# Side products of a two-layer attention kernel in four column groups, with a new schedule for them

## The chip, the cores and the metric

The kernel runs on one core of a Trainium2 chip. The metric is the device time of one execution in microseconds (us). The core has a matrix engine (TensorE, PE in the profile, with its weight loads as PEld), a vector engine (VectorE, DVE), a scalar engine (ScalarE, ACT), a general engine (GpSimd, POOL), a queue engine that issues transfers (SyncE, SP), and 16 DMA engines. Matmul results go to PSUM, eight banks of 128 x 512 floats.

## The reference, cut to what matters

Two layers on x of shape (4, 256, 64, 64), all float32. Layer 0 ("A") is attention of every pixel to 1024 keys that come from 2x2 convolutions; layer 1 ("B") is attention within four areas of 1024 pixels each, plus a 7x7 depthwise convolution of the values, and a projection.

```python
# layer 0: x = x + L0(_gn(x));  8 heads of 32, scale 32**-0.5
q = einsum('oc,bchw->bohw', Wq, x)                  # 4096 queries an image
k, v = conv2x2_stride2(x, Wk), conv2x2_stride2(x, Wv)   # 1024 keys and values
attn = softmax((q.k + q.(rel_h + rel_w)) * scale);  out = attn @ v
# layer 1: x = x + L1(_gn(x))
q, k, v = conv1x1(x, w_qkv)                         # in 4 areas of 1024 pixels
out = softmax(q.k * scale) @ v                      # within an area
out = conv1x1(out + dwconv7(v, w_pe), w_proj)       # 49 taps
# _gn: normalization over 32 groups of channels, of the whole image
```

## The kernel before

The program is a list of 128 units in eight blocks of 16 (A of images 0, 1, 2, then B0, A3, B1, B2, B3). A unit is 512 queries of four heads. It has eight steps, one for each 128 keys. In each step TensorE makes the scores (`s`), ScalarE exponentiates them into two tiles `p`, and a step later TensorE adds up the weighted values in one bank (`av`). The four heads share the array: scores lie in four row groups (32 x 128), the sums of v and of the exponentials (`den`, the divisors) in four column groups (128 x 32).

```python
def weighted(unit, j, p, av):
    v = unit[3]()
    for h in range(4):
        T.matmul(
            av[HD * h : HD * h + HD, :], lhsT=v[:, j, unit[0] * P + HD * h : unit[0] * P + HD * h + HD],
            rhs=p[h // 2][:, h % 2, :], start=(j == 0), stop=(j == NKT - 1),
        )
```

All else TensorE does (keys, values and queries of both layers, the projection, the values for the convolution) is a side task. A task is a generator that yields after each piece of its matmuls; all of them use the full array (128 x 128). A piece is two matmuls of 512 columns or four of 256. Tasks take one of three pairs of banks (`s`) that the scores use too.

```python
def make_k(a, qd):                       # of layer 1; the others look alike
    ...
    k, ps = kvs["k"], ps_pair(f"k1ps_{b}_{a}_{qd}")
    for half in range(2):
        for t in range(CT):
            T.matmul(
                ps[:, half, :], lhsT=wqkv_sb[:, t, 1, qd * P : (qd + 1) * P],
                rhs=hs[a][:, t, half * CH : (half + 1) * CH], start=(t == 0), stop=(t == CT - 1),
            )
        if half == 0:
            yield
    S.activation(...)                    # PSUM to SBUF
```

The main loop. `advance()` runs one piece of the oldest task; `need()` runs pieces until a result that is wanted is there.

```python
while now[0] < last or plan or later or side:
    g, j = divmod(now[0], NKT)
    if now[0] < last:
        if j == 0:
            ps = {}
        ps[j] = scores(units[g], j)
    do(g, j)                             # what the plan has for this step; tasks go to side
    for _ in range(1 + (len(side) > 2)):
        if side:
            advance()
    if before is not None:
        weighted(*before)
        if j == 0:
            avs[g - 1] = pool.tile([P, CH], FP, tag="av", name="av_sb", bufs=2)
            S.copy(avs[g - 1], before[3])
    ...
```

The divisors: outside the time of the convolutions (`free`) VectorE adds all eight steps' exponentials and one divisor group follows in step 1 of the next unit. While VectorE works at the convolutions (units 22 to 123) it makes five adds a unit, GpSimd issues folding DMAs (`accum_op`), and three divisor groups follow in steps 1, 2 and 3.

```python
    free = g + 1 < begin or g > start
    if free:
        if j:
            add(0, 0, j)
            add(1, 0, j)
        groups = [(9, 0, 0)]
    else:
        if j % 2:
            fold(j - 1, j)
        if j == 3:
            soon(3, lambda: fold(0, 2))
        if j % 3:
            add(1, j - j % 3, j)
        groups = [(9, 0, 0), (10, 4, 3), (11, 6, 6)]
```

Dividing: the divisors are copied to `den_sb`, sent through memory into a narrow tile (`rows`, `few`), inverted there, sent back and spread (`recs`, `rb`), and multiplied over a unit later. The convolution is 49 multiply-adds on VectorE into one accumulator (`acc`, one buffer), for each of four images, two halves and two channel blocks, 6.3 units apart from unit 22.3 on. ScalarE normalizes in `normalize`, VectorE gathers statistics with bn_stats. x is read in chunks of 512 KB: once for the statistics (`xs`), again for keys and values (`xa`), for queries (`hq`) and for the residual (`xc`).

Of the kernel before, what the change touches and what calls it, by code (L numbers as in the profile page):

```python
# [15 lines left out]
P = 128  # L16
B, C, HH, WW = 4, 256, 64, 64
N = HH * WW
CT = C // P
# [31 lines left out]
def direct_path(  # L51
# [50 lines left out]
    S.dma_start(wv0_sb, wv0.rearrange("(t p) k o -> p t k o", p=P))  # L102
    S.dma_start(wq0_sb, wq0.rearrange("(t p) o -> p t o", p=P))
    relh_sb = const.tile([P, CT, 32], FP, name="relh_sb")
    relw_sb = const.tile([P, CT, 32], FP, name="relw_sb")
    S.dma_start(relh_sb, relh.rearrange("(t p) j -> p t j", p=P))
    S.dma_start(relw_sb, relw.rearrange("(t p) j -> p t j", p=P))
    G.dma_start(wqkv_sb, wqkv.rearrange("(t p) k o -> p t k o", p=P))
    G.dma_start(wp_sb, wproj.rearrange("(t p) o -> p t o", p=P))
    wpe_sb = const.tile([P, CT, NTAP], FP, name="wpe_sb")  # L110
    G.dma_start(wpe_sb, wpe.rearrange("(t p) k -> p t k", p=P))
    bqkv_sb = const.tile([P, 3, CT], FP, name="bqkv_sb")
    G.dma_start(bqkv_sb, bqkv.rearrange("k (t p) -> p k t", p=P))
    bpe_sb = const.tile([P, CT], FP, name="bpe_sb")
    G.dma_start(bpe_sb, bpe.rearrange("(t p) -> p t", p=P))
    bproj_sb = const.tile([P, CT], FP, name="bproj_sb")
    G.dma_start(bproj_sb, bproj.rearrange("(t p) -> p t", p=P))

    bpv_sb = const.tile([P, CT], FP, name="bpv_sb")
    V.tensor_add(bpv_sb, bpe_sb, bqkv_sb[:, 2, :])  # L120
# [169 lines left out]
    def plan_a(b, u, prep):  # L290
# [4 lines left out]
        seen = {}  # L295

        def look(c):
            seen[c] = first[c] if b == 0 and c < len(first) else load_chunk(b, c, "xs")

        def add_stats(c):  # L300
            for t in range(CT):
# [21 lines left out]
        def make_k(a):  # L323
            if a == 0:
                taps["k"] = k_tile(key)
            k, ps = taps["k"], ps_pair(f"k0ps_{b}_{a}")
            for qd in range(2):
                for n in range(8):
                    t, i, w = n // 4, n // 2 % 2, n % 2
                    T.matmul(  # L330
                        ps[:, qd, :256], lhsT=wk0_sb[:, t, 2 * i + w, qd * P : (qd + 1) * P],
                        rhs=taps[a][:, t, i, w], start=(n == 0), stop=(n == 7),
                    )
                    if n == 3 or n == 7 and qd == 0:
                        yield
            S.copy(k[:, :, a * 256 : (a + 1) * 256], ps[:, :, :256])  # L336
            if a == NAREA - 1:

                for qd in range(2):
                    rows = k[:, qd, :].rearrange("p (i j) -> p i j", j=32)  # L340
                    V.tensor_add(rows, rows, relh_sb[:, qd : qd + 1, :].to_broadcast([P, 32, 32]))
                    V.tensor_add(rows, rows, relw_sb[:, qd, :].unsqueeze(2).to_broadcast([P, 32, 32]))
                ks[key] = k

        def make_v(a):
            if a == 0:
                taps["v"] = v_tile(key)
            v, ps = taps["v"], ps_pair(f"v0ps_{b}_{a}")
            for m in range(2):
                for n in range(8):  # L350
                    t, i, w = n // 4, n // 2 % 2, n % 2
                    T.matmul(  # L352
                        ps[:, m, :C], lhsT=taps[a][:, t, i, w, m * P : (m + 1) * P],
                        rhs=wv0_sb[:, t, 2 * i + w, :], start=(n == 0), stop=(n == 7),
                    )
# [26 lines left out]
        def make_q(c):  # L382
            hq = hqs.pop(c)
            q = pool.tile([P, 2, CH], FP, tag="q", name=f"q0_{b}_{c}", bufs=2)
            ps = ps_pair(f"q0ps_{b}_{c}")
            for qd in range(2):
                for t in range(CT):
                    T.matmul(  # L388
                        ps[:, qd, :], lhsT=wq0_sb[:, t, qd * P : (qd + 1) * P], rhs=hq[:, t, :],
                        start=(t == 0), stop=(t == CT - 1),  # L390
                    )
                if qd == 0:
                    yield
            S.copy(q, ps)  # L394
            qs["A", b, c] = q
# [33 lines left out]
    def plan_b(b, u):  # L429
# [14 lines left out]
        def make_k(a, qd):  # L444
            if qd == 0:
                kvs["k"] = k_tile(("B", b, a))
            k, ps = kvs["k"], ps_pair(f"k1ps_{b}_{a}_{qd}")
            for half in range(2):
                for t in range(CT):
                    T.matmul(  # L450
                        ps[:, half, :], lhsT=wqkv_sb[:, t, 1, qd * P : (qd + 1) * P],
                        rhs=hs[a][:, t, half * CH : (half + 1) * CH], start=(t == 0), stop=(t == CT - 1),
                    )
                if half == 0:
                    yield
            S.activation(
                k[:, qd, :].rearrange("p (h n) -> p h n", h=2), ps, AF.Identity, bias=bqkv_sb[:, 1, qd : qd + 1]
            )
            if qd == 1:
                ks["B", b, a] = k  # L460

        def make_v(a, half):
# [4 lines left out]
            for m in range(4):  # L467
                kt = 4 * half + m
                for t in range(CT):
                    T.matmul(  # L470
                        ps[:, m, :], lhsT=hs[a][:, t, kt * P : (kt + 1) * P],
                        rhs=wqkv_sb[:, t, 2, :], start=(t == 0), stop=(t == CT - 1),
                    )
# [6 lines left out]
        def make_q(c):  # L480
            q = pool.tile([P, 2, CH], FP, tag="q", name=f"q1_{b}_{c}", bufs=2)
            ps = ps_pair(f"q1ps_{b}_{c}")
            for qd in range(2):
                for t in range(CT):
                    T.matmul(  # L485
                        ps[:, qd, :], lhsT=wqkv_sb[:, t, 0, qd * P : (qd + 1) * P],
                        rhs=hs[c // 2][:, t, (c % 2) * CH : (c % 2 + 1) * CH],
                        start=(t == 0), stop=(t == CT - 1),
# [30 lines left out]
        def project(c):  # L519
            cv, xm = rest[c]  # L520
            ps = ps_pair(f"ops_{b}_{c}")
            for to in range(CT):
                for t in range(CT):
                    T.matmul(  # L524
                        ps[:, to, :], lhsT=wp_sb[:, t, to * P : (to + 1) * P], rhs=cv[:, t, :],
                        start=(t == 0), stop=(t == CT - 1),
                    )
# [28 lines left out]
    def plan_values(b, c, start):  # L556
# [11 lines left out]
        def values():  # L568
            h = made.pop("h")
            ps = ps_pair(f"vals_ps_{b}_{c}")  # L570
            for t in range(CT):
                for tt in range(CT):
                    T.matmul(  # L573
                        ps[:, t, :], lhsT=wqkv_sb[:, tt, 2, t * P : (t + 1) * P], rhs=h[:, tt, :],
                        start=(tt == 0), stop=(tt == CT - 1),
                    )
# [11 lines left out]
    def plan_conv(b, half, t, start, pace):  # L588
# [58 lines left out]
    for b in range(B):  # L647
        assert start >= ends[b] + 6.0
        for c in range(NCH):
            plan_values(b, c, start - 3.7 + 0.4 * c if c < 5 else start + 3.0 * (c - 4))  # L650
        for half in range(2):
            for t in range(CT):
                plan_conv(b, half, t, start, pace)
# [19 lines left out]
        tc.manual_schedule(engines={engines.PE, engines.Activation, engines.DVE, engines.Pool, engines.SP})  # L673
    )

    def sum_up(g, j, ps):
# [3 lines left out]
        free = g + 1 < begin or g > start  # L680
        if free:

            if j:
                add(0, 0, j)
                add(1, 0, j)
# [18 lines left out]
    while now[0] < last or plan or later or side:  # L704
# [629 lines left out]
```

## Time and profile before

| | before |
|---|---|
| time, median of three runs | 3722.2 us (3713.27 to 3727.89) |
| span in the profile | 3716.5 us |
| instructions | 55404 |
| first scores of unit 0 start at | 94.4 us |
| last copy of a sum of v (av_sb) starts at | 3676.6 us |
| last copy of divisors (den_sb) starts at | 3680.9 us |

How to read it: the page gives each engine's busy time and its share of the span. A group is one line of the program with one pair of tiles; its mean is that of one instruction. A float32 matmul appears as two instructions (two passes), so eight `av` instructions are the four heads of one step. Matmuls overlap, so their durations don't add up: what a group costs is read from its start to the next group's start. The costliest groups, as line, engine, operation, tiles, count, busy us and mean ns, and the idle time before them:

```profile
L237 ACT ACTIVATE p<-s 128x1024 f32<-128x1024 f32 x2048 | 1991.2, 1026 | 968.5 <-PE s L232 794.9
L616 DVE SCALAR_TENSOR_TENSOR acc<-vin,wpe_sb,acc 128x1984 f32<-128x1984 f32 (+12 forms) x768 | 1714.0, 2232 | 6.3
L678 DVE TENSOR_TENSOR p<-p 128x1024 f32<-128x1024 f32 x874 | 1045.2, 1220 | 322.4 <-PE av L244 147.0
L679 POOL DMA_DIRECT2D p<-p x510 | 445.0, 930 | 2513.6 <-ACT p L237 778.2
L470 PE MATMUL v1ps<-wqkv_sb,h 128*128 128x256 f32 x512 | 128.3, 394 | 0.0
L573 PE MATMUL vals_ps<-hv,wqkv_sb 128*128 128x512 f32 x256 | 126.8, 618 | 1.2 <-ACT p L237 0.8
```

The first is ScalarE's exponentials, the second VectorE's taps, the third its adds, the fourth the folding DMAs. The last two are two of the eight kinds of side products.

### The profile page before, as it was taken

To read this page: it belongs to the slowest core of one execution; us is meant where nothing else is said; L and a number is where in the kernel's file an instruction comes from. 1 tells how busy PE (TensorE), PEld (TensorE's weight loads), DVE (VectorE), ACT (ScalarE), POOL (GpSimd) and SP (SyncE) were. 2 spreads that over 40 slices of the span, in tenths; PEclk is the share of its full clock that TensorE was granted. 3 is DMA by queue.
4 is the path that set the end of the run, shared out by engine and by line. 5 is a ranking of instruction groups with operands and counts; after the bars stand their busy time and mean duration, and the time that the engine had idled before them with its cause. 6 is when DMAs were issued, how large, how long until landed. Compare 5 with 4: busy or idle time off the path is not lost.

```text
span 3716.5 us, 55404 instructions
## 1 busy us (share of the span) xinstructions
PE 3536.4 (95%) x21890; PEld 1136.7 (31%) x21890; DVE 3030.7 (82%) x2326; ACT 2533.3 (68%) x2929; POOL 475.2 (13%) x550
## 2 busy tenths in 40 slices
PE   6999999999989999999999999999999999999996
PEld 5223432234222232233432222323233233333221
DVE  1897487985988969897679987989796989898965
ACT  2887677765666666676567776667676777766774
POOL 0000000111111111211111111111111111111110
PEclk9999999999999999999999999999999999999998
DMA  4112123775667776777557787666776676767651
GB/s 157 56 59 70 49 84 114 160 184 119 144 149 167 162 175 157 180 157 169 128 123 179 175 190 173 139 159 145 171 170 172 141 178 162 167 140 167 140 132 53
DMA packets 233885, 531.03 MB, mean 143 GB/s; under 512 B 62400, under 2 KB 64704, under 8 KB 233616
## 3 DMA queue, kind: packets, MB, share of 16 engines
q0 software_dynamic: 73792, 268.52, 38.1%
q1 hardware_dynamic: 158464, 256.46, 21.2%
q8 instruction: 173, 2.83, 0.3%
q10 hardware_dynamic: 1360, 2.43, 0.2%
q14 instruction: 96, 0.79, 0.1%
HBM read 190.70 MB, written 69.21 MB: 70 GB/s over the span
## 4 chain that ended last, share of the span: by engine, by line
PE 77%; DMA 8%; issue 5%; ACT 4%; DVE 4%; SPq 1%; POOL 0%; DVEq 0%; ACTq 0%; POOLq 0%
PE s L232 24%; PE av L244 21%; PE den L254 7%; DMA p<-p 4%; PE v1ps L470 3%; PE ops L524 3%; PE k1ps L450 3%; PE k0ps L330 3%; PE q1ps L485 3%; PE vals_ps L573 3%; PE q0ps L388 3%; PE v0ps L352 3%; DVE p L678 2%; ACT p L237 2%; DVE acc L616 1%
## 5 line engine op out<-in xcount | busy, mean ns | idle before, releaser
L237 ACT ACTIVATE p<-s 128x1024 f32<-128x1024 f32 x2048 | 1991.2, 1026 | 968.5 <-PE s L232 794.9
L616 DVE SCALAR_TENSOR_TENSOR acc<-vin,wpe_sb,acc 128x1984 f32<-128x1984 f32 (+12 forms) x768 | 1714.0, 2232 | 6.3
L678 DVE TENSOR_TENSOR p<-p 128x1024 f32<-128x1024 f32 x874 | 1045.2, 1220 | 322.4 <-PE av L244 147.0
L679 POOL DMA_DIRECT2D p<-p x510 | 445.0, 930 | 2513.6 <-ACT p L237 778.2
L232 PE MATMUL s<-q,k_A 32*128 32x512 f32 x4096 | 652.2, 655 | 17.3 <-ACT q L394 10.7
L232 PE MATMUL s<-q,k_B 32*128 32x512 f32 x4096 | 613.4, 641 | 1.0 <-ACT q L493 0.8
L244 PE MATMUL av<-p,v_A 128*32 128x512 f32 x4096 | 557.6, 612 | 29.1 <-ACT av_sb L718 28.2
L244 PE MATMUL av<-p,v_B 128*32 128x512 f32 x4096 | 547.1, 606 | 5.9 <-ACT av_sb L718 5.9
L254 PE MATMUL den<-p,ones 128*32 128x512 f32 x2656 | 370.3, 610 | 46.4 <-DMA p<-p 35.8
L232 PEld LDWEIGHTS s<-q,k_A 32*128 32x128 f32 x4096 | 196.7, 186 | 479.1 <-issue 201.6
L232 PEld LDWEIGHTS s<-q,k_B 32*128 32x128 f32 x4096 | 184.0, 183 | 435.9 <-ACT p L237 165.5
L244 PEld LDWEIGHTS av<-p,v_A 128*32 128x32 f32 x4096 | 81.8, 108 | 398.1 <-issue 322.8
L244 PEld LDWEIGHTS av<-p,v_B 128*32 128x32 f32 x4096 | 80.8, 108 | 358.6 <-issue 326.3
L254 PEld LDWEIGHTS den<-p,ones 128*32 128x32 f32 x2656 | 86.7, 112 | 269.0 <-issue 184.8
L524 PE MATMUL ops<-cv,wp_sb 128*128 128x512 f32 x256 | 130.6, 635 | 17.9 <-DVE cv L517 13.0
L450 PE MATMUL k1ps<-h,wqkv_sb 128*128 128x512 f32 x256 | 127.6, 621 | 3.0 <-ACT p L237 3.0
L330 PE MATMUL k0ps<-taps,wk_sb 128*128 128x256 f32 x512 | 126.0, 394 | 4.5 <-ACT taps L215 4.5
L470 PE MATMUL v1ps<-wqkv_sb,h 128*128 128x256 f32 x512 | 128.3, 394 | 0.0
L573 PE MATMUL vals_ps<-hv,wqkv_sb 128*128 128x512 f32 x256 | 126.8, 618 | 1.2 <-ACT p L237 0.8
L485 PE MATMUL q1ps<-h,wqkv_sb 128*128 128x512 f32 x256 | 127.0, 618 | 0.6 <-ACT hv L580 0.6
L352 PE MATMUL v0ps<-wv_sb,taps 128*128 128x256 f32 x512 | 124.7, 391 | 2.6 <-ACT k_A L336 2.6
L388 PE MATMUL q0ps<-hq,wq_sb 128*128 128x512 f32 x256 | 126.5, 620 | 0.0
(83 smaller groups left out, 1536.9 us busy)
## 6 DMA issues: line engine op xcount, KB each, us to landing
p<-p POOLq DMA_DIRECT2D x510, 512.0 KB, 5.7
rb<-recs SPq DMA_DIRECT2D x512, 64.0 KB
xs<-in_x SPq DMA_DIRECT2D x32, 512.0 KB
xa<-in_x SPq DMA_DIRECT2D x32, 512.0 KB
hq<-in_x SPq DMA_DIRECT2D x32, 512.0 KB
xc<-in_x SPq DMA_DIRECT2D x32, 512.0 KB
xmid<-xc SPq DMA_DIRECT2D x32, 512.0 KB
hv<-xmid SPq DMA_DIRECT2D x32, 512.0 KB
```

The lines of the kernel that those rows point to most:

```text
L232: T.matmul(pairs[h // 2][:, h % 2, :], lhsT=k[rows, unit[0], j * P : (j + 1) * P], rhs=q[rows, :], start=True, stop=True,)
L237: S.activation(p[i], pairs[i], AF.Exp, scale=SCALE)
L244: T.matmul(av[HD * h : HD * h + HD, :], lhsT=v[:, j, unit[0] * P + HD * h : unit[0] * P + HD * h + HD], rhs=p[h // 2][:, h % 2, :], start= ...
L254: T.matmul(dens[g][HD * h : HD * h + HD, :], lhsT=ones, rhs=(p[0], q[1])[h // 2][:, h % 2, :], start=first, stop=last,)
L450: T.matmul(ps[:, half, :], lhsT=wqkv_sb[:, t, 1, qd * P : (qd + 1) * P], rhs=hs[a][:, t, half * CH : (half + 1) * CH], start=(t == 0), sto ...
L470: T.matmul(ps[:, m, :], lhsT=hs[a][:, t, kt * P : (kt + 1) * P], rhs=wqkv_sb[:, t, 2, :], start=(t == 0), stop=(t == CT - 1),)
L485: T.matmul(ps[:, qd, :], lhsT=wqkv_sb[:, t, 0, qd * P : (qd + 1) * P], rhs=hs[c // 2][:, t, (c % 2) * CH : (c % 2 + 1) * CH], start=(t == ...
L524: T.matmul(ps[:, to, :], lhsT=wp_sb[:, t, to * P : (to + 1) * P], rhs=cv[:, t, :], start=(t == 0), stop=(t == CT - 1),)
L573: T.matmul(ps[:, t, :], lhsT=wqkv_sb[:, tt, 2, t * P : (t + 1) * P], rhs=h[:, tt, :], start=(tt == 0), stop=(tt == CT - 1),)
L616: V.scalar_tensor_tensor(dst, src, w, dst, ALU.mult, ALU.add)
L678: add = lambda i, to, j: soon(1, lambda: V.tensor_add(ps[to][i], ps[to][i], ps[j][i]))
L679: fold = lambda to, j: G.dma_start(ps[to][0], ps[j][0], accum_op=ALU.add)
```

## The change

It has five parts. Side products are split into four column groups of 32, so that they have the shape of the sums of v (`product`). Side tasks get a piece in five steps of a unit only, chosen so that they avoid the steps with divisors, and more when tasks pile up. The first image's chunks all stay on chip in the buffers of `p`, so its second read (`xa`) goes away, and all weights are read after it by the same queue. The last unit divides with a reciprocal over the whole tile instead of the way through memory. The convolutions' taps are squeezed into 5.7 of their 6.3 units, and the first values for images 1 to 3 are made earlier and further apart.

```diff
-    first = [load_chunk(0, c, "xs") for c in range(4)]
+    first = [pool.tile([P, CT, CH], FP, tag="p", name=f"first_{c}", bufs=13) for c in range(NCH)]
+    for c in range(NCH):
+        nc.sync.dma_start(first[c], xv[0][:, :, c * CH : (c + 1) * CH])
 ...
-    S.dma_start(wk0_sb, wk0.rearrange("(t p) k o -> p t k o", p=P))
+    nc.sync.dma_start(wk0_sb, wk0.rearrange("(t p) k o -> p t k o", p=P))
 ... (the other weights alike, from S and G to nc.sync)
+    def product(out, lhsT, rhs, start, stop):
+        for i in range(4):
+            cols = slice(HD * i, HD * i + HD)
+            T.matmul(out[cols, :], lhsT=lhsT[:, cols], rhs=rhs, start=start, stop=stop)
 ... (in divide)
+        if g == len(units) - 1:
+            rb = pool.tile([P, CH], FP, tag="p", name="rb", bufs=13)
+            V.reciprocal(rb, den_sb)
+            V.tensor_mul(unit[4]()[:, unit[0], :], avs.pop(g), rb)
+            V.tensor_reduce(sums[:, 0, g : g + 1], den_sb, AX.X, ALU.add)
+            V.tensor_reduce(sums[:, 1, g : g + 1], rb, AX.X, ALU.add)
+            return
 ... (in plan_a)
-            areas[a] = [load_chunk(b, 2 * a + half, "xa") for half in range(2)]
+            areas[a] = [first[2 * a + half] if b == 0 else load_chunk(b, 2 * a + half, "xa") for half in range(2)]
 ... (in make_k, make_v, make_q of both layers, project, values)
-                    T.matmul(
+                    product(
 ... (in plan_conv)
-            at(0, when((pace - 0.3) * n / NTAP), lambda dy=dy, dx=dx: tap(dy, dx))
-        at(0, when(pace - 0.3), store)
+            at(0, when((pace - 0.6) * n / NTAP), lambda dy=dy, dx=dx: tap(dy, dx))
+        at(0, when(pace - 0.6), store)
 ...
-            plan_values(b, c, start - 3.7 + 0.4 * c if c < 5 else start + 3.0 * (c - 4))
+            plan_values(b, c, start - (7.5 - 1.2 * c if b else 3.7 - 0.4 * c) if c < 5 else start + 3.0 * (c - 4))
 ... (in the main loop)
-        for _ in range(1 + (len(side) > 2)):
+        rooms = (0, 2, 4, 5, 7) if free(g) else (0, 4, 5, 6, 7)
+        for _ in range((j in rooms or len(side) > 2) + (len(side) > 4)):
             if side:
                 advance()
```

More of the change, by code (lines that the diff above doesn't have):

```diff
@@ L100, in direct_path @@
     wp_sb = const.tile([P, CT, C], FP, name="wp_sb")
-    S.dma_start(wk0_sb, wk0.rearrange("(t p) k o -> p t k o", p=P))
-    S.dma_start(wv0_sb, wv0.rearrange("(t p) k o -> p t k o", p=P))
-    S.dma_start(wq0_sb, wq0.rearrange("(t p) o -> p t o", p=P))
+    nc.sync.dma_start(wk0_sb, wk0.rearrange("(t p) k o -> p t k o", p=P))
+    nc.sync.dma_start(wv0_sb, wv0.rearrange("(t p) k o -> p t k o", p=P))
+    nc.sync.dma_start(wq0_sb, wq0.rearrange("(t p) o -> p t o", p=P))
     relh_sb = const.tile([P, CT, 32], FP, name="relh_sb")
     relw_sb = const.tile([P, CT, 32], FP, name="relw_sb")
[L106 to L109, printed above, removed]
+    nc.sync.dma_start(relh_sb, relh.rearrange("(t p) j -> p t j", p=P))
+    nc.sync.dma_start(relw_sb, relw.rearrange("(t p) j -> p t j", p=P))
+    nc.sync.dma_start(wqkv_sb, wqkv.rearrange("(t p) k o -> p t k o", p=P))
+    nc.sync.dma_start(wp_sb, wproj.rearrange("(t p) o -> p t o", p=P))
     wpe_sb = const.tile([P, CT, NTAP], FP, name="wpe_sb")
-    G.dma_start(wpe_sb, wpe.rearrange("(t p) k -> p t k", p=P))
+    nc.sync.dma_start(wpe_sb, wpe.rearrange("(t p) k -> p t k", p=P))
     bqkv_sb = const.tile([P, 3, CT], FP, name="bqkv_sb")
-    G.dma_start(bqkv_sb, bqkv.rearrange("k (t p) -> p k t", p=P))
+    nc.sync.dma_start(bqkv_sb, bqkv.rearrange("k (t p) -> p k t", p=P))
     bpe_sb = const.tile([P, CT], FP, name="bpe_sb")
-    G.dma_start(bpe_sb, bpe.rearrange("(t p) -> p t", p=P))
+    nc.sync.dma_start(bpe_sb, bpe.rearrange("(t p) -> p t", p=P))
     bproj_sb = const.tile([P, CT], FP, name="bproj_sb")
-    G.dma_start(bproj_sb, bproj.rearrange("(t p) -> p t", p=P))
+    nc.sync.dma_start(bproj_sb, bproj.rearrange("(t p) -> p t", p=P))
     bpv_sb = const.tile([P, CT], FP, name="bpv_sb")
@@ L297, in look @@
         def look(c):
-            seen[c] = first[c] if b == 0 and c < len(first) else load_chunk(b, c, "xs")
+            seen[c] = first[c] if b == 0 else load_chunk(b, c, "xs")
         def add_stats(c):
@@ L351, in make_v @@
                     t, i, w = n // 4, n // 2 % 2, n % 2
-                    T.matmul(
+                    product(
                         ps[:, m, :C], lhsT=taps[a][:, t, i, w, m * P : (m + 1) * P],
@@ L387, in make_q @@
                 for t in range(CT):
-                    T.matmul(
+                    product(
                         ps[:, qd, :], lhsT=wq0_sb[:, t, qd * P : (qd + 1) * P], rhs=hq[:, t, :],
@@ L449, in make_k @@
                 for t in range(CT):
-                    T.matmul(
+                    product(
                         ps[:, half, :], lhsT=wqkv_sb[:, t, 1, qd * P : (qd + 1) * P],
@@ L469, in make_v @@
                 for t in range(CT):
-                    T.matmul(
+                    product(
                         ps[:, m, :], lhsT=hs[a][:, t, kt * P : (kt + 1) * P],
@@ L484, in make_q @@
                 for t in range(CT):
-                    T.matmul(
+                    product(
                         ps[:, qd, :], lhsT=wqkv_sb[:, t, 0, qd * P : (qd + 1) * P],
@@ L523, in project @@
                 for t in range(CT):
-                    T.matmul(
+                    product(
                         ps[:, to, :], lhsT=wp_sb[:, t, to * P : (to + 1) * P], rhs=cv[:, t, :],
@@ L572, in values @@
                 for tt in range(CT):
-                    T.matmul(
+                    product(
                         ps[:, t, :], lhsT=wqkv_sb[:, tt, 2, t * P : (t + 1) * P], rhs=h[:, tt, :],
@@ L674, in direct_path, with free @@
     )
+    def free(g):
+        return g + 1 < begin or g > start
     def sum_up(g, j, ps):
@@ L679, in sum_up @@
         fold = lambda to, j: G.dma_start(ps[to][0], ps[j][0], accum_op=ALU.add)
-        free = g + 1 < begin or g > start
-        if free:
+        if free(g):
             if j:
```

## The prediction

> **What bounds the kernel now.** I read the page's engine line and its chain first:
>
> ```profile
> PE 3536.4 (95%) x21890; PEld 1136.7 (31%) x21890; DVE 3030.7 (82%) x2326; ACT 2533.3 (68%) x2929; POOL 475.2 (13%) x550
> PE 77%; DMA 8%; issue 5%; ACT 4%; DVE 4%; SPq 1%; POOL 0%; DVEq 0%; ACTq 0%; POOLq 0%
> ```
>
> TensorE is the bound, VectorE stands second. Busy time of matmuls that overlap says little, so I took durations from start to start in TensorE's timeline. Columns: start, length, engine, line, operation, tiles, shape, count.
>
> ```profile
> 3044.62 1.14 PE L232 MATMUL s<-q,k_B 32*128 32x512 f32 x8
> 3045.69 1.07 PE L244 MATMUL av<-p,v_B 128*32 128x512 f32 x8
> 3046.58 1.04 PE L254 MATMUL den<-p,ones 128*32 128x512 f32 x8
> 3047.55 1.14 PE L232 MATMUL s<-q,k_B 32*128 32x512 f32 x8
> 3048.62 1.07 PE L244 MATMUL av<-p,v_B 128*32 128x512 f32 x8
> 3049.61 1.31 PE L232 MATMUL s<-q,k_B 32*128 32x512 f32 x8
> ...
> 3057.91 1.14 PE L232 MATMUL s<-q,k_B 32*128 32x512 f32 x8
> 3058.98 1.98 PE L573 MATMUL vals_ps<-hv,wqkv_sb 128*128 128x512 f32 x4
> 3060.89 1.06 PE L244 MATMUL av<-p,v_B 128*32 128x512 f32 x8
> 3061.89 1.14 PE L232 MATMUL s<-q,k_B 32*128 32x512 f32 x8
> ```
>
> A plain step (s to s) is 2.06 us, one with a divisor group 2.93, one with a piece of side work 3.98. The av group takes 0.89 before den, which has the same shape, and 0.99 before s: a change of shape costs about 0.1 us. Four passes of a full-array piece need 1.72 us in a long row of them (16 matmuls of 256 columns, 32 passes, in 6.91 us at the start), but 1.91 between s and av.
>
> The starts of all s groups give 1024 steps. The undisturbed ones have medians of 2.07, 2.93, 3.98 and 4.85 (side and divisors). There are 456 steps with side work (479 pieces; some 34 more lie before the first unit) and 331 divisor groups. So TensorE's own work from first to last s is 1023 x 2.07 + 331 x 0.86 + 456 x 1.91 + 23 x 1.72 = 3313 us. The measured stretch is 3577: 264 us are waits and throttled clock. Of these 123 lie in step 1 of the units, about 54 where av waits for the copy of the last sum out of its only bank, 48 where the first divisor group waits for a folding DMA. The waits also show a stop of VectorE:
>
> ```profile
> PE av L244 <- ACT av_sb L718: 34.1, 59, 3.9
> PE den L254 <- DMA p<-p: 35.8, 19, 3.9
> DVE acc L613 <- DMA conv<-acc: 80.2, 10, 18.3
> ```
>
> (us in total, times, longest). VectorE's room is read stage by stage (stretch, us, busy of PE, PEld, DVE, ACT, POOL, clock, DMA share, GB/s):
>
> ```profile
> 94.40:353.10 258.70, 253.13 (x1696) 67.40 (x1696) 224.44 (x236) 216.18 (x244) 2.51 (x3) 0.99 0.18 58
> 663.50:799.50 136.00, 125.66 (x800) 32.93 (x800) 134.75 (x93) 96.24 (x113) 21.88 (x25) 0.92 0.72 158
> 2871.50:3592.40 720.90, 716.42 (x4492) 220.95 (x4488) 623.74 (x428) 505.95 (x571) 112.46 (x130) 1.00 0.70 158
> ```
>
> These are units 0 to 11, 22 to 27 and 97 to 123. In the last TensorE never rests and VectorE has 13% free: 24.0 us of a 27.7 us unit. In the second VectorE is full.
>
> [...] the second pass's four loads follow 7 ns apart while the first streams. [...] four column groups quadruple the instructions: a piece with 256 columns becomes 32 loads and 32 matmuls in 1.72 us, 54 ns for a pair. The kernel's last product, after an empty queue, shows the pace:
>
> ```profile
> 3703.16 0.11 PEld L735 LDWEIGHTS count<-ones,least 128*1 128x1 f32 x2 [4.16 <-issue]
> 3703.19 0.19 PE L735 MATMUL count<-ones,least 128*1 128x1 f32 x2 [3.37 <-DVE least L733]
> ```
>
> Mean matmul there is 163 ns, so the second starts 27 ns after the first, its load included. [...] 54 ns fits. [...]
>
> **The change, part by part.**
>
> 1. Column groups. A piece in the shape of av and den, next to av, should cost what two divisor groups cost, 2 x 0.86 = 1.72, against 1.91. Saving 0.19 x 456 = 87 us. For 256 columns, the same if issue keeps up. Before the first unit pieces already run back to back at full pace: no gain.
>
> 2. Rooms. A side step lasts 3.98 us, while ScalarE needs only 2 x 1.03 us for its exponentials; a plain step leaves it none. Before, side pieces often fall in the divisor steps (141 steps of 4.96 us on average) and 381 steps are plain. In units with three divisor groups, rooms 0, 4, 5, 6, 7 leave about one plain step; a piece in step 0 also gives ScalarE the time to copy av before step 1. I take off about half of the av waits (27 us), a third of the fold waits (16) and 20 of the remaining 141 us, mostly plain steps at ScalarE's pace. Sum 63.
>
> 3. Convolution pace. A convolution's 49 taps now take 5.7 instead of 6.0 units, and the gap before the next grows from 0.3 to 0.6 units (some 16 us), which should swallow the 80 us of VectorE waiting for conv<-acc (longest 18.3). But while taps run, VectorE needs 49/5.7 x 2.15 (start to start of taps) = 18.5 plus some 8.3 of adds, multiplies and statistics = 26.8 us a unit. TensorE's unit in the last stage will be 27.7 - 4.27 x 0.19 = 26.9. In units with few side pieces (22 to 27, 36 to 48, 64 to 79) TensorE would be at 24 to 26 and VectorE binds; averaged over the gap it needs (49 x 2.15 + 6.3 x 8.3)/6.3 = 25.0. I charge 0.3 us on the 32 units concerned, 10 us.
>
> 4. First image, weights. The eight chunks are read first, without weights beside them and without waiting for six buffers. Now:
>
> ```profile
> 20.32 5.40 DVE L302 BATCH_NORM_STATS2 st_A<-xs 128x6 f32<-128x512 f32 x8 [0.29 <-DMA xs<-in_x]
> 32.84 8.70 PE L330 MATMUL k0ps<-taps,wk_sb 128*128 128x256 f32 x32 [4.49 <-ACT taps L215]
> ```
>
> From 7 to 14 us the transfers ran at 369 GB/s (the stretch's view), but shared between x and the weights. At that rate x alone, 4.2 MB, takes 11.4 us and arrives by about 14, so statistics end near 15.5 instead of 25.6. TensorE then starts near 22.5 and the rest follows unchanged: 10 us saved. The second read of this image for the taps (xa) is hidden already.
>
> 5. Last unit. From den_sb (3680.9) to the multiply (3690.3) four DMA hops pass, and the next add waits for cv until 3692.5. A reciprocal of 512 columns in their place: 16 columns take 246 ns, a plain two-column operation 160, so about 6 to 8 ns a column and an estimated 3 to 4.4 us, then 0.7 for the product and 1.2 for the two sums. Saved: 5 us.
>
> Total: 87 + 63 - 10 + 10 + 5 = 155, so 3722 - 155 = 3567; I say 3562, as fewer steps of mixed shape also shorten what ScalarE and VectorE wait for.
>
> **Rivals.** (a) VectorE takes over: it is full in units 22 to 27, and everything behind a late tap, adds and so divisors, is late too. For it: busy 0.99 there; the denser taps. Against: 0.86 elsewhere, and its 80 us stop goes. If it binds all conv units at 26.8, about 100 units x 26.8 = 2680 where 2929 are spent now less the dense stages, the gain outside TensorE's own 87 us vanishes: 3620 to 3650. (b) Issue or weight loads bind the 256-column pieces: 150-odd pieces in steps; at twice the planned pace each would lose 1.7 us, 260 us in all with the start's, and the kernel would be slower, near 3800. The 27 ns pair speaks against it. (c) Side work held back by the rooms is then forced in one burst when its unit begins, and a task that waits across steps 1 to 3 keeps one of three pairs of banks, so that s waits for ScalarE some 0.3 us a step: up to 60 us lost, near 3620. The doubling when more than two or four tasks queue speaks against it. (d) Most of the 264 us of waits go with the new spacing: 3480.
>
> **Range and chances.** Column groups alone are worth 87 us or 2.3%, start and tail 15; the waits can go either way by 60 to 80. So 3562, with 3485 to 3640 for 8 in 10. Faster by over 2% (below 3648): 0.86; within 2%: 0.10; slower: 0.04, nearly all of it (b).
>
> **What would show it.** Right: side steps of 3.79 us and divisor-with-side steps rare; the k0ps rows at the start still 6.9 us for their 16 products; TensorE starting near 22 us; conv<-acc gone from VectorE's waits; TensorE still over 95% busy in units 97 to 123 at near 27 us each. Wrong: side pieces with 256 columns far longer than those with 512 (b); den waiting for VectorE's adds, and VectorE above 0.95 in the conv stages (a); s waiting for ScalarE in steps 1 to 3, or steps with three pieces and more (c).

## The result and the profile after

The changed kernel takes **3633.5 us** (median of four runs, 3628.6 to 3637.7) against 3724.0 for the kernel before beside it: a ratio of **0.976, 95% interval 0.9736 to 0.9785**, so 80 to 98 us less. The prediction said 3562, with 3485 to 3640. The direction holds, and the range by 6.5 us; some 70 us of the expected 160 did not come. In the profiled runs the spans are 3716.5 and 3636.0 us, 80.5 apart. Line numbers have moved by 9 to 20 from one kernel to the other.

The engine line of the page, after:

```profile
PE 3450.4 (95%) x30338; PEld 1007.4 (28%) x30338; DVE 3035.4 (83%) x2327; ACT 2530.9 (70%) x2929; POOL 471.5 (13%) x544
```

The page counts 8448 matmuls more, as side products come in quarters, and TensorE is as full as before. VectorE and ScalarE do the same work in a shorter span.

The timeline of TensorE, after: a side piece with 256 columns and one with 512.

```profile
460.49 1.14 PE L241 MATMUL s<-q,k_A 32*128 32x512 f32 x8
461.56 1.93 PE L150 MATMUL k0ps<-taps,wk_sb 128*32 128x256 f32 x32
463.31 1.04 PE L253 MATMUL av<-p,v_A 128*32 128x512 f32 x8
464.28 1.14 PE L241 MATMUL s<-q,k_A 32*128 32x512 f32 x8
...
2960.84 1.93 PE L150 MATMUL q1ps<-h,wqkv_sb 128*32 128x512 f32 x16
2962.58 1.04 PE L253 MATMUL av<-p,v_B 128*32 128x512 f32 x8
```

From the piece's start to av's it is 1.75 us for 256 columns and 1.74 for 512 (before 1.91), and av takes 0.97 before s (before 1.00). The whole step, s to s, is 3.79 us where it was 3.98.

The starts of single passes show where these 0.20 us go (medians over 199 undisturbed steps with 512 columns before and 223 after). From the piece's last pass to av it is 0.43 us instead of 0.52, the pass's own length, as the shape no longer changes there: 0.09 saved. From av's first pass to its second it is 0.43 instead of 0.45: 0.02 saved. From the piece's first pass to its second it is 0.45 instead of 0.53, although the shape still changes before it: 0.08 saved. A weight load takes 0.11 us with 32 columns and 0.19 with 128, and the s groups, which load 128, keep 0.53 there; that the shorter load is the reason is my reading.

The waits, after (us in total, times, longest). A weight load (PEld) that waits may still lie beside running matmuls: for av_sb the loads wait 145.4 us and the matmuls 46.2.

```profile
PEld s L241 <- ACT p L246: 437.4, 508, 12.2
PEld av L253 <- ACT av_sb L738: 145.4, 123, 4.8
PE av L253 <- ACT av_sb L738: 46.2, 81, 3.9
PEld den L263 <- DMA p<-p: 29.8, 14, 4.3
```

Waits of av for the copy of the last sum have grown (as matmuls 34.1 to 46.2 us), those of the divisors for folding DMAs have shrunk (as weight loads 57.2 to 29.8). VectorE's 80.2 us of waiting for conv<-acc no longer stand in this view; the most that its convolution waits for one transfer is now 26.1 us in total, for vin<-vals.

Units 22 to 27 and 97 to 123, after, in the view by stretches whose columns the prediction names:

```profile
655.00:786.00 131.00, 120.44 (x920) 31.14 (x920) 130.51 (x91) 95.80 (x113) 21.88 (x25) 0.97 0.74 162
2811.90:3514.10 702.20, 697.16 (x6120) 198.28 (x6120) 620.23 (x427) 507.48 (x572) 113.00 (x130) 1.00 0.72 162
```

The late units last 27.0 us (702.2/26) with TensorE busy for 99% of them, as expected. VectorE is full in the early stage, 130.5 of 131.0 us. The other signs for being right came too: steps with a divisor group and a piece are rare (11, before 145), and the products of the start take 6.91 us, but for the first. So did one sign for being wrong, that of rival (c): seven steps carry three pieces and more (before five, of three at most), and the time lost in step 3 of the convolutions' units to s waiting for ScalarE rises from 8 to 18 us.

The start, after. The first image's statistics end at 15.7 us, ten sooner, and the first keys start at 22.8 instead of 32.8. Their first product takes 9.4 us where it took 8.5, so the first scores start only 9.2 us sooner:

```profile
11.67 4.00 DVE L318 BATCH_NORM_STATS2 st_A<-first 128x6 f32<-128x512 f32 x6
22.78 9.54 PE L150 MATMUL k0ps<-taps,wk_sb 128*32 128x256 f32 x128 [4.48 <-ACT taps L224]
```

**Where the time went.** The same count as in the prediction, from the starts of the s groups, splits each profiled run in four. "Work" is the number of steps of each kind times its undisturbed length (a side piece now costs 1.717 us instead of 1.91, an additional one 1.72); "waits" is the measured stretch less that, so it contains half-clock time too. A few pieces can be counted either way, which leaves some 5 us open in these two rows.

| us | before | after | predicted change | measured |
|---|---|---|---|---|
| start to first s | 94.4 | 85.2 | -10 | -9.2 |
| TensorE's work, first to last s | 3312.9 | 3221.7 | -87 | -91.2 |
| waits, first to last s | 264.3 | 283.3 | -63, and +10 for the pace | **+19.0** |
| last s to the copy of the last divisors | 9.3 | 10.4 | | +1.1 |
| from that copy to the end | 35.6 | 35.4 | -5 | **-0.2** |

The work did what it should. The waits and the end did not, and the experiments ask why.

### The profile page after: what moved, and what is told of

It is laid out like the page before. It is cut to its first block, busy times and chain, and to the rows that moved or that the text cites. A ratio compares the mean times of both kernels' runs of the same rounds, so it can differ in the third digit from the quotient of the medians.

```text
span 3636.0 us, 72301 instructions
## 1 busy us (share of the span) xinstructions
PE 3450.4 (95%) x30338; PEld 1007.4 (28%) x30338; DVE 3035.4 (83%) x2327; ACT 2530.9 (70%) x2929; POOL 471.5 (13%) x544
## 5 line engine op out<-in xcount | busy, mean ns | idle before, releaser
L241 PE MATMUL s<-q,k_A 32*128 32x512 f32 x4096 | 655.7, 651 | 43.4 <-ACT p L246 23.8
L253 PEld LDWEIGHTS av<-p,v_A 128*32 128x32 f32 x4096 | 98.5, 110 | 384.1 <-issue 285.9
L253 PEld LDWEIGHTS av<-p,v_B 128*32 128x32 f32 x4096 | 108.8, 109 | 326.5 <-issue 249.8
L150 PE MATMUL ops<-cv,wp_sb 128*32 128x512 f32 x1024 | 126.4, 613 | 17.2 <-DVE cv L533 13.8
L150 PE MATMUL k0ps<-taps,wk_sb 128*32 128x256 f32 x2048 | 123.4, 387 | 4.5 <-ACT taps L224 4.5
L150 PE MATMUL vals_ps<-hv,wqkv_sb 128*32 128x512 f32 x1024 | 123.1, 598 | 1.8 <-ACT p L246 1.8
L150 PE MATMUL q1ps<-h,wqkv_sb 128*32 128x512 f32 x1024 | 124.3, 605 | 0.0
L150 PE MATMUL v1ps<-wqkv_sb,h 128*32 128x256 f32 x2048 | 123.8, 382 | 0.0
L150 PE MATMUL k1ps<-h,wqkv_sb 128*32 128x512 f32 x1024 | 123.2, 598 | 0.0
L150 PE MATMUL q0ps<-hq,wq_sb 128*32 128x512 f32 x1024 | 121.7, 597 | 0.0
L150 PE MATMUL v0ps<-wv_sb,taps 128*32 128x256 f32 x2048 | 119.6, 386 | 0.0
```

Source lines behind the costliest of these rows:

```text
L150: T.matmul(out[cols, :], lhsT=lhsT[:, cols], rhs=rhs, start=start, stop=stop)
L241: T.matmul(pairs[h // 2][:, h % 2, :], lhsT=k[rows, unit[0], j * P : (j + 1) * P], rhs=q[rows, :], start=True, stop=True,)
L253: T.matmul(av[HD * h : HD * h + HD, :], lhsT=v[:, j, unit[0] * P + HD * h : unit[0] * P + HD * h + HD], rhs=p[h // 2][:, h % 2, :], start= ...
```

## The experiments

All twelve ran beside the kernel before. The theories, by the letters that the expectations use: R, the new rooms give about half of what is gained besides the column groups; V, VectorE's load in the convolution stages sets the waits; C, step 1 has lost its side piece, and the copy of av is uncovered there; B, rooms pile side pieces up and give them out in bursts; F, the first divisor group waits for a folding DMA; A, ScalarE's turn at the copy of av holds av back; E, the earlier values bring the rest.

**1. The column groups alone.** The kernel before with `product()` and nothing else:

```diff
-                    T.matmul(
+                    product(
```

> The kernel before with the column groups alone: old places for side pieces, old start, old end, old convolution pace. Counted from the traces, TensorE's own work falls by 92 us. Theory V (VectorE is full in 59 of the 101 convolution units after the change, so a part of what TensorE saves comes back as waits): 3640 to 3665. If the whole saving is kept: 3632. Theory R (the column groups give about half and the new rooms the other half): about 3680.

3642.0 us, ratio 0.9776 (0.9760 to 0.9793): 80.5 us less than before, most of the whole gain. Work falls by 88.0 us to 3224.9, waits rise by 12 to 276: some of the time that TensorE gains is spent waiting for what it doesn't produce.

**2. Everything but the column groups.**

```diff
     def product(out, lhsT, rhs, start, stop):
-        for i in range(4):
-            cols = slice(HD * i, HD * i + HD)
-            T.matmul(out[cols, :], lhsT=lhsT[:, cols], rhs=rhs, start=start, stop=stop)
+        T.matmul(out, lhsT=lhsT, rhs=rhs, start=start, stop=stop)
```

> The changed kernel with full-array side products again; all its other parts stay. Theory V: the rooms give nothing that lasts, so this is the kernel before less 9 us at the start, 3700 to 3725. Theory R: 3655 to 3680, as the rooms then bring about half of the gain or the 63 us of waits that were predicted.

3701.6 us, 0.9946 (0.9930 to 0.9962). All other parts together are worth 21 us, and the column groups 68 on top of them. Waits are 257 here.

**3. The changed kernel with the old rooms**, one piece in any step and two when over two tasks queue:

```diff
-        for _ in range((j in rooms or len(side) > 2) + (len(side) > 4)):
+        for _ in range(1 + (len(side) > 2)):
```

> The changed kernel with a side piece in every step again, divisor steps included. Theory V: 3620 to 3650, no difference beyond 0.5%, as waits on VectorE decide. Theory R: 3680 to 3700, as the 63 us of waits come back. If the rooms do harm (step 1 never has a side piece that could cover the copy of av): below 3620.

3613.5 us, 0.9699 (0.9681 to 0.9717), clearly faster than the changed kernel. The rooms **cost 20 us**; theory R is false. Waits are 263, against 283 with the rooms, and the tail is 28.8 us against 35.4. The waits with the old rooms:

```profile
PEld s L241 <- ACT p L246: 327.7, 391, 4.3
PEld av L253 <- ACT av_sb L738: 86.6, 63, 4.8
PEld den L263 <- DMA p<-p: 50.6, 25, 5.7
```

The rooms cut the third by two fifths (to 29.8), as planned, and pay with the other two. s waits for ScalarE when the pair of banks it is to write is still being read. This line is 290 to 328 us in the six kernels with the old rooms and 401 to 440 in those with the new ones, save one (375, number 8).

Of the 20 us of waits, 7 lie in units 11 to 16 (33.1 us a unit against 34.6), where keys and values of layer 0 are made, and 12 in unit 28 alone, most of them in one step of the changed kernel:

```profile
809.12 2.14 ACT L224 ACTIVATE taps<-xa,norm_A 128x256 f32<-128x256 f32 x4 [7.08 <-DMA xa<-in_x]
817.90 2.98 PE L241 MATMUL s<-q,k_A 32*128 32x512 f32 x8 [11.32 <-ACT p L246]
```

ScalarE is to normalize a chunk (xa) that has not landed, and the exponentials stand behind it in order. Two parts of the change do this together. The rooms put no pieces into steps 1 to 3, so step 5, for which the normalization is planned, starts 16.9 us after its unit does (22.7 with the old rooms). And with the squeezed taps a convolution ends in this unit just ahead of the read of xa: in SyncE's queue the read stands behind the stores of conv and the loads of vin, and goes out only after 20.7 us. The unit loses 15 us here and 7 to 9 in numbers 2, 5, 6 and 8, which have both parts. It loses 3 with the old rooms, 3 with the old pace (number 7, where the read goes out after 12.6 us), and 3 with half the taps (4 and 9).

The tail explains part 5. In the changed kernel:

```profile
3601.22 3.35 DVE L276 RECIPROCAL rb<-den_sb 128x512 f32<-128x512 f32 x1 [1.77 <-ACT den_sb L273]
3606.40 1.21 DVE L552 TENSOR_TENSOR xm<-xm,cv 128x1024 f32<-128x1024 f32 x1
...
3608.09 0.47 SPq L528 DMA_DIRECT2D cv<-conv  x1
3613.01 1.22 DVE L533 TENSOR_TENSOR cv<-cv,att_B 128x1024 f32<-128x1024 f32 x1 [4.79 <-DMA cv<-conv]
```

With the old rooms:

```profile
3578.36 1.22 DVE L552 TENSOR_TENSOR xm<-xm,cv 128x1024 f32<-128x1024 f32 x1
3584.49 3.35 DVE L276 RECIPROCAL rb<-den_sb 128x512 f32<-128x512 f32 x1 [2.64 <-ACT den_sb L273]
3590.39 1.22 DVE L533 TENSOR_TENSOR cv<-cv,att_B 128x1024 f32<-128x1024 f32 x1
```

The direct division does save 6.8 us (35.6 before, 28.8 here). In the changed kernel the rooms hold back the projection of the last chunk but one, so that its add (xm) falls behind the reciprocal on VectorE. The store of its result stands behind that add, and the load of cv behind the store, in SyncE's queue; the last sum waits 4.8 us for that load.

**4. Every second tap of the convolution left out** (24 of the 49; the centre stays), so the output lacks them; all else as in the changed kernel:

```diff
         for n, (dy, dx) in enumerate(taps):
-            at(0, when((pace - 0.6) * n / NTAP), lambda dy=dy, dx=dx: tap(dy, dx))
+            if n % 2 == 0:
+                at(0, when((pace - 0.6) * n / NTAP), lambda dy=dy, dx=dx: tap(dy, dx))
```

> The changed kernel with every second tap of the convolution left out (25 of 49 are made, at their old places); the output lacks them. VectorE is relieved of 384 taps of 2.15 us, 826 us. Theory V: TensorE's waits fall from 283 us to 120 to 170, time 3470 to 3520. Theory S (the waits are those of the schedule: the copy of av before step 1, plain steps at ScalarE's pace, bursts): waits stay above 230, time 3580 to 3630.

3595.8 us, 0.9653 (0.9631 to 0.9676). VectorE falls from 83% to 62% of the span, and in the early stage, where it was full, to 70% (86.9 of 125.0 us, from 655 to 780).

Yet only 37 us go, and 246 us of waits stay. VectorE's load is a contributor and not the cause; theory V is false as it stood, and both ranges of theory S hold. Some 15 us of the gain are time at half clock with TensorE at work, which falls from 43 to 28 us between the first and the last s (the mean granted clock of the profiled runs is 0.983 in the changed kernel and 0.988 here). What the kernel before would gain from the same relief was not run, so the 37 us are not a share of the 70 that the prediction missed.

**5. A side piece put back in step 1**, where av waits for the copy, in place of step 0:

```diff
-        rooms = (0, 2, 4, 5, 7) if free(g) else (0, 4, 5, 6, 7)
+        rooms = (1, 2, 4, 5, 7) if free(g) else (1, 4, 5, 6, 7)
```

> The changed kernel with step 1 in place of step 0 among the five steps in which side pieces are given out. Theory C (the rooms lost 20 us against a piece in every step because nothing stands between scores and av in step 1 any more, where av waits for the copy out of its bank: 66 us of such waits in the convolution's stretch against 40): those waits fall back to about 40 and the time to 3600 to 3618. Theory B (the loss comes from pieces held back and then run seven to nine in a row before a unit): no change, 3625 to 3640.

3650.4 us, 0.9804 (0.9775 to 0.9832): slower by 17 us. The waits for the copy did fall back to what they were before, as theory C says: as weight loads 84.1 us, 61 times, where the changed kernel has 145.4 and 123. In the convolution stages the steps lost to them fall from 65 to 36 us, but those lost to folds rise from 23 to 38 and all waits from 283 to 299. C names a real wait and does not explain the time.

**6. The order of the divisor groups swapped**, so that the first one takes the pair of tiles that needs no folding DMA of the last step:

```diff
-        groups = [(9, 0, 0), (10, 4, 3), (11, 6, 6)]
+        groups = [(9, 4, 3), (10, 0, 0), (11, 6, 6)]
```

> The changed kernel with the first two of the three divisor groups in the other order: the one that needs the second-level fold, issued at step 6, comes in step 2 instead of step 1. Theory F (the fold is simply late for step 1[...]): the 23 us of waits for the folding DMA in step 1 vanish[...], 3600 to 3618. If they only move to step 2 or to VectorE's adds for the other group: 3625 to 3640.

3628.7 us, 0.9745 (0.9718 to 0.9773), not to be told from the changed kernel. The fold waits of step 1 all but vanish (23 us to 1), but total waits fall only by 10, in part because s waits longer for ScalarE two steps later (18 to 24 us).

**7. The old pace of the taps** (6.0 units instead of 5.7 for a convolution):

```diff
-            at(0, when((pace - 0.6) * n / NTAP), lambda dy=dy, dx=dx: tap(dy, dx))
-        at(0, when(pace - 0.6), store)
+            at(0, when((pace - 0.3) * n / NTAP), lambda dy=dy, dx=dx: tap(dy, dx))
+        at(0, when(pace - 0.3), store)
```

> The changed kernel with the convolution's taps over 6.0 units and a gap of 0.3 again. As predicted for this part: VectorE's stops for conv<-acc, 80 us, come back, and the taps are less dense: 3630 to 3650. If the denser taps cost more than the stops: 3610 to 3628.

3630.1 us, 0.9753 (0.9729 to 0.9778): no difference. The squeeze neither helps nor harms, although VectorE's waits for conv<-acc are back here, 75.6 us.

**8. Tasks drained one earlier**, against the bursts. In the changed kernel six steps carry seven to nine pieces and last 15 to 19 us; before, three pieces were the most.

```diff
-        for _ in range((j in rooms or len(side) > 2) + (len(side) > 4)):
+        for _ in range((j in rooms or len(side) > 1) + (len(side) > 4)):
```

> The changed kernel with pieces given out in every step as soon as two tasks wait (before: three), so fewer pieces are held back. Theory B (the rooms' loss of 20 us comes from pieces held back and run seven to nine in a row before a unit, while ScalarE and VectorE stand): 3613 to 3626, and the six steps with seven or more pieces become fewer. If bursts don't matter: 3628 to 3640.

3633.3 us, 0.9747 (0.9728 to 0.9766): the same. But the bursts only shrank to five to seven pieces, so the run doesn't settle theory B. The six steps themselves hold 9.5 us of waits. The run does speak on the other half of rival (c), the pair of banks that a half-done task keeps. The order of the matmuls shows that with the old rooms no step passes without a piece while a task is half done; in the changed kernel 92 such steps lose 20 us, and here 22 lose 9, while the time stays.

**9. ScalarE relieved of the copy of av**, on top of number 4 (the same taps left out), so that VectorE has room for it:

```diff
-            S.copy(avs[g - 1], before[3])
+            V.tensor_copy(avs[g - 1], before[3])
```

> The changed kernel with every second tap left out (the output lacks them), and the copy of the finished av bank made by VectorE, which then has room, in place of ScalarE. Against 3596 us and 246 us of waits with half the taps alone. Theory A (in a plain step ScalarE has 2.05 us of exponentials and in step 0 also 0.59 us of this copy, while TensorE needs 2.07 us; its work in a row sets the waits): the 47 us of waits before av in step 1 go, waits 185 to 210, time 3540 to 3565. If waits only move elsewhere: 3580 to 3600.

3609.0 us, 0.9688 (0.9670 to 0.9706), 13 us more than number 4. In units 22 to 123 waits fall by 13 us; before unit 22 and at the end, where VectorE has all the adds, they rise by 20. Theory A fares like C: the wait moves. But av's waits for the copy are only cut, as weight loads from 129.4 to 108.1 us, and not gone as A asks, so this is a weak test of it.

**10. A version put together from what had helped**: old rooms, swapped groups, and the last chunk's second read two units earlier.

```diff
-            at(g + 3, 2, lambda c=c: load_rest(c))
+            at(g + 3 - 2 * (b == 3 and c == NCH - 1), 2, lambda c=c: load_rest(c))
-        groups = [(9, 0, 0), (10, 4, 3), (11, 6, 6)]
+        groups = [(9, 4, 3), (10, 0, 0), (11, 6, 6)]
-        for _ in range((j in rooms or len(side) > 2) + (len(side) > 4)):
+        for _ in range(1 + (len(side) > 2)):
```

> Column groups, a side piece in every step as before, the two divisor groups swapped, and the last unit's reads of conv and xmid issued two units earlier. Against 3613 with a piece in every step: the 47 us of fold waits go (theory F) and 6 us at the end, as the add no longer waits for cv behind the reciprocal: 3560 to 3580. If fold waits only move: 3600 to 3612. The stretch from the last copy of the divisors to the end, 35.4 us in the changed kernel, should be 28 to 31.

**3601.7 us, 0.9666 (0.9644 to 0.9688)**, the fastest of all with the whole computation, 32 us below the changed kernel and 123 below before. Waits are 258:

```profile
PEld av L253 <- ACT av_sb L738: 99.2, 62, 12.8
PEld den L263 <- DMA p<-p: 6.5, 7, 2.9
```

The swap takes nearly all waits for folds (50.6 us in number 3), and all waits still fall by 5 us only: those for the copy of av rise from 86.6 to 99.2 (as matmuls from 35.6 to 49.0), 12.8 of them in one wait. The earlier read brought nothing: the tail is 29.5 us, against 28.8 with the old rooms alone. Against those its interval overlaps a little (0.9681 to 0.9717), so the 12 us between their medians are likely, not certain.

**11. Number 10 with the normalizations on GpSimd** (hq, hv and h), to relieve ScalarE:

```diff
-                normalize(key, hqs[c][:, t, :], hqs[c][:, t, :], t)
+                normalize_pool(key, hqs[c][:, t, :], hqs[c][:, t, :], t)   # G.tensor_scalar(mult, add); hv and h alike
```

> The fastest version so far (3602 us: column groups, a piece in every step, swapped divisor groups, last reads earlier) with 135 us of normalizations (hq, hv and h) moved from ScalarE to GpSimd. Theory A: 3565 to 3592. If GpSimd delays the folding DMAs it issues, or ScalarE isn't what TensorE waits for: 3600 to 3650.

3633.0 us, 0.9750 (0.9733 to 0.9767), 31 us slower. The group in the page's manner:

```profile
L224 POOL TENSOR_SCALAR hv<-hv,norm_B 128x512 f32<-128x512 f32 x64 | 161.2, 2554 | 14.6 <-issue 7.6 <-DVE st_A L322 5.1 <-DMA hv<-xmid 2.0
```

One takes 2554 ns on average on GpSimd, 812 on ScalarE before. Units 16 to 22, before the folds begin, do get shorter than in number 10 (24.5 to 23.8 us); the units with convolutions lose 36 us more to waits. GpSimd, which also issues the folding DMAs, issues them 0.1 to 0.4 us later on average, but TensorE's waits for them don't grow (6.4 us as weight loads, 6.5 in number 10); the products of the values wait 14.8 us in total, seven times, for the slow normalization. As one engine is relieved and a slower one put into the way, the run says little on theory A.

**12. The old rooms and also the values as before**, to find what lies between numbers 1 and 3:

```diff
-            plan_values(b, c, start - (7.5 - 1.2 * c if b else 3.7 - 0.4 * c) if c < 5 else start + 3.0 * (c - 4))
+            plan_values(b, c, start - 3.7 + 0.4 * c if c < 5 else start + 3.0 * (c - 4))
```

> The kernel after with the old rooms (3613.5 us) and, besides, the first five values of every image planned as before (from 3.7 units ahead of the convolutions, 0.4 units apart). The column groups, the start, the squeezed taps and the last unit stay as after. Between the column groups alone (3642.0) and the old rooms (3613.5) lie 29 us, of which 9 are the start. Theory E (the earlier and wider values bring the rest): the time rises by about 20 us to 3633, waits from 263 to about 280, in the stages in which the values for images 1 to 3 are made. Rival (the values' timing brings nothing, the rest is a matter of chance in how the program falls together): 3610 to 3617.

3621.7 us, 0.9721 (0.9704 to 0.9737). The values' new timing brings 8 us, not 20, and as the intervals of this run and number 3 overlap, it may be less. Waits are 276 here, as in number 1, and 263 in number 3. Between numbers 1 and 12 lie 20.3 us of the medians and 16.5 of the profiled spans: 9.9 from the earlier start and 6.7 from the tail; the squeezed taps are in this difference too.

## Why the prediction was right, and where it was wrong

The medians now close step by step: 3722.5 before (beside number 1), less 80.5 for the column groups, 20.3 for start and last unit together (with the squeezed taps), 8.2 for the values, plus 20.0 for the rooms, is 3633.5.

**Part 1, column groups: right.** Expected 87 us; 88.0 us of work went (number 1). A piece in av's shape costs what two divisor groups cost, and one change of shape falls away. That accounts for some 0.12 us of the 0.20 saved in a step; 0.08 lie at the start of the piece itself, where the shape still changes, and the prediction did not name them. The profile shows what a change of shape costs: av starts 0.43 us after the last pass of a piece of its own shape and 0.52 after one of the other. Rival (b) is dead: 256 columns cost 1.75 us with 32 loads and 32 matmuls, like 512, so issue keeps up at 54 ns for a pair. What the step missed is that 12 of the 88 us come back as waits (number 1).

**Part 2, rooms: the step that failed.** The prediction put it as "I take off about half of the av waits (27 us), a third of the fold waits (16) and 20 of the remaining 141 us ... Sum 63". Each of these waits was real, but they were added up as if each could be taken away alone. The fold waits did fall (48 to 23 us in step 1). The waits for the copy of av were to fall by 27 us and rose by as much in the convolution stages (39 to 65). The mechanism was right: "a piece in step 0 also gives ScalarE the time to copy av", and the 33 units with a piece in step 0 alone lose 0.2 us in all. But a piece in step 1 had done the same in 61 of these 102 units before, and the rooms took it away. Units with a piece in neither step lose about 1 us each, and there are now 66 of them instead of 41, as step 0 gets only 0.3 to 0.4 pieces a unit. And s waits more for ScalarE, 12 us of it in unit 28, where the faster first steps bring ScalarE to a load that has not landed. In all the rooms cost 20 us where 63 were to be gained (23 in the profiled runs: 20 of waits and 7 of the tail, less 4 elsewhere). Of the four rivals (c) comes nearest: side work held back, bursts of up to nine pieces, s waiting for ScalarE. The bursts come because the queries that the next unit needs stand in the queue behind up to eight pieces of keys and values. Taking away most of the steps with a held pair of banks (number 8) left the time as it was; what the bursts cost beyond their own 9.5 us stays open.

**Part 3, pace: of no consequence.** The stop at conv<-acc went and VectorE binds in units 22 to 27 (busy for 130.5 of 131.0 us), both as predicted; but number 7 shows that the pace makes no difference in sum. What the squeeze costs in unit 28 together with the rooms is made up elsewhere. The 10 us charged are within what can't be told.

**Part 4, start: right**, 9.2 us for 10; the keys did start 10.1 us sooner.

**Part 5, last unit: right in its mechanism, void in this kernel.** Expected 5 us, and 6.8 measured without the rooms. With them the next add's inputs came late, 0.2 us in all. The reciprocal took 3.35 us, within the estimate of 3 to 4.4.

Rival (d) fell, and (a) is at most a part: with half of the taps gone 246 us of waits remain, and no version had fewer. The measured time lies in the range of (a), but its sum does not lead there: 2680 us, which VectorE would need, are 249 less than the 2929 spent. That the prediction's range held, by 6.5 us, is owed to the room it left for the waits and not to the schedule it foresaw; its point, 3562, rests on the 63 us of part 2. In the kernels run here the waits lie between 246 and 299 us whatever single cause is taken away. When the copy (5, 9), the fold (6) or VectorE's load (4) is relieved, another wait takes most of the place. That TensorE, ScalarE and VectorE are tied in a loop with three pairs of banks for s and one bank for av, so that the next link binds, is how I read it; which link would have to be widened is not shown.

## What to carry to other kernels

When a matmul shape alternates with a small one, splitting the large product into the small one's shape can be worth more than it costs in instructions (88.0 us of TensorE's work in number 1; 8448 more matmuls in the page after); read both shapes' start-to-start times from the trace first. Waits of a pipeline in balance are not to be added up as savings: take the one that ends last away in a run of its own and look for what takes its place. And when a schedule shifts side work, look at what queues behind it at the end: here the last sum waited 4.8 us for a load that stood behind a store in SyncE's queue.

## What was not expected of the hardware

**Waits cost twice.** Between the first and the last s the granted clock falls to one half 20 times before and 19 times after, for 3.4 or 6.8 us, once for 13.7. All 19 idle times of TensorE over 2.7 us in the two traces (by the modelled ends of its matmuls) come with such a fall, and 20 of the 39 between 1.5 and 2.7 us. The timeline of the changed kernel, ScalarE and TensorE:

```profile
2188.70 1.02 ACT L246 ACTIVATE p<-s 128x1024 f32<-128x1024 f32 x1 [3.58 <-DVE p L698]
2190.26 1.94 PE L253 MATMUL av<-p,v_A 128*32 128x512 f32 x8 [3.95 <-ACT av_sb L738]
```

VectorE's add kept ScalarE waiting 3.6 us for a buffer of p, so the copy came late, TensorE waited 3.95 us, and then its eight matmuls took 1.94 us instead of 1.04; from 2188.4 to 2195.2 us the granted clock was 0.50. Within a trace the starts of the falls lie whole multiples of 3.4133 us apart, to 0.02 us. In the 3.41 us before a fall TensorE was without a matmul for 1.4 to 3.4 us. What decides whether a wait brings a fall is not shown. In all, 67 us of clock were lost so before and 63 after (14 and 12 of them at the end), none in units 97 to 123 (granted clock 1.00 in both kernels), where no wait brings a fall. Between the first and the last s TensorE was at work for 47 and 43 us of the time lost, so I estimate that some 45 of the 264 and 283 us of waits are their echo.

**GpSimd's normalization is three times as slow as ScalarE's** in number 11, 2554 to 812 ns on average for hv's 128 x 512 floats and 2511 to 820 for hq's; for h's 128 x 1024 it is 2870 to 1237.
